# Adds of a routed unit's tiles into the output without waits between them, with spare rows for each tile

## The chip, the cores and the metric

The kernel runs on one core of a Trainium2 chip. The metric is the device time of one execution in microseconds (us). A profiled execution also has a span, from the first to the last instruction that the profile records; the device time is a little longer than the span. The engines are named as in the profile: PE (TensorE, matmuls), PEld (its weight loads), DVE (VectorE), ACT (ScalarE), POOL (GpSimd) and SP (SyncE, which here only issues DMAs). A name such as POOLq is the engine's sequencer, which handles waits and branches.

## What is computed

Four sequences of 512 tokens of 256 numbers go through a gated feed-forward stage with one expert of weights for each sequence, attention with 16 query heads over one shared key and value head, and a residual. Then comes a routed feed-forward layer with 8 experts, whose result is added to the output:

```
x = x + attn(cond(x))                      # (4, 512, 256)
xg = mixed(x).reshape(8 groups, 256 tokens, 256)
probs = softmax(xg @ w_router)             # 8 experts; each token chooses its best 2
each group sends at most 128 tokens to an expert (capacity)
h = gelu(tokens_of_expert @ wi[e])         # 256 -> 1024
y = h @ wo[e]                              # 1024 -> 256
out[token] = x[token] + sum over its chosen experts of probs[token, e] * y
```

So every token is handled by up to two experts, and its output row gets up to two additions on top of the row that the attention stage wrote.

## The kernel before

**Stages.** Up to about 390 us the kernel computes the gated feed-forward stage, the projections and the attention of the four sequences, interleaved, and scatters each token's row into a DRAM table `xp` sorted by expert (`scattered` and `numbered`, L826 to L863, by indirect DMAs from POOL at L850). From about 383 us on it runs the routed units.

**Routed units.** A unit (`routed`, L1064) is a run of rows of one expert in `xp`: 256 rows for "first", "early" and "pair" units, and 96 to 320 rows (`SIZES`, L38) for the eight "last" units, which take what is left of each expert. The list of units is at L1376 to L1380; the very last unit, ("last", 3) with 224 rows, has buffers of its own (names ending in `_alone`) and runs after a conditional block. A unit loads its expert's weights `wi` and `wo` and its rows `xt`, turns the rows by PE transposes into `xTr` (L1143, copied by DVE at L1147), makes `h` in `up` (PE at L1170, ACT at L1174) and the result in `put` (PE at L1236 into `psC`). `go` (L1258) runs `up` of unit t, the transposes of unit t+1, then `put` of unit t-1, so `put` lags by one unit. A unit has two or three tiles of up to 128 rows: 320 rows are 128, 128 and 64; 224 are 128 and 96; 192 are 128 and 64.

**Handing a tile over.** For each tile `i` of `m` rows, `out` (L1206) calls `weights` (L1189): five tiny DVE instructions (L1195 to L1199) that compute each row's factor `w0` and the output row `at` to which it is added. A row of `xp` that holds no token has the number 0; for those `at` points to spare rows behind the 2048 rows of the output: row 2048 + p for partition p, from the constant `spare1` (L211), one column for every tile. A tile of at most 64 rows also has two halves added (L1210, L1211). Then DVE scales the result into `y` (L1213) and POOL issues an indirect DMA that adds `y` to the output rows in DRAM (L1216, `compute_op=ALU.add`). After the last tile the adds end in DRAM and the program ends.

**What orders the adds.** The scheduler takes every indirect DMA into `out_rows` as touching all of it, so each add waits for the landing of the add before it, by a semaphore wait on POOL ahead of the DMA. Without that wait two adds could work on the same row at the same time: rows of one expert are different tokens, but the spare rows are shared by all tiles, and a token's two experts are in different units. `apart` (L276) takes a dependence away for a named group; `behind` (L279) adds one by hand. `y`, `at` and the factors have two buffers each in turn (pool `fp`), so a unit's DVE work waits for the adds of the unit two before it.

**The conditional block.** At L1477 every engine reads the flag `over`, and at L1478 a block for rows that did not fit is skipped in this input. Behind it, `last_go` runs the last unit. On the skipping path POOL first waits until all its earlier DMAs have landed, then sets its DMA semaphores to what the block would have left.

```
a = nc.gpsimd.indirect_dma_start(                     # L1216, in out()
    out=out_rows,
    out_offset=bass.IndirectOffsetOnAxis(ap=at[0:m, i : i + 1], axis=0),
    in_=y[0:m, i, :],
    in_offset=None,
    compute_op=ALU.add,
)
```

Of the kernel before, what the change touches and what calls it, by code (L numbers as in the profile page):

```python
# [9 lines left out]
F32 = mybir.dt.float32  # L10
# [4 lines left out]
ALU = mybir.AluOpType  # L15
# [3 lines left out]
P = 128  # L19
B = 4  # L20
T = 512
NT = B * T
D = 256
# [32 lines left out]
def adaln_attn_ffn_kernel(  # L56
# [21 lines left out]
    nc = tc.nc  # L78
# [63 lines left out]
    rows = const.tile([1, B], I32, name="rows")  # L142
# [59 lines left out]
    def numbers(name, shape, pattern, base, step):  # L202
        t = const.tile(shape, F32, name=name)
        nc.gpsimd.iota(
            t, pattern=pattern, base=base, channel_multiplier=step,
            allow_small_or_imprecise_dtypes=True,
        )
        return t

    token1 = numbers("token1", [P, NCH], [[P, NCH]], 1, 1)  # L210
    spare1 = numbers("spare1", [P, 1], [[0, 1]], NT + 1, 1)  # L211
    free = numbers("free", [P, NE], [[EROWS, NE]], 0, 0)
    begin = numbers("begin", [P, NE, NG], [[EROWS, NE], [P, NG]], 0, 0)
    tens = numbers("tens", [P, NE, 4], [[0, NE], [2, 4]], 2, 0)
# [25 lines left out]
    for n in range(2):  # L240
        t = const.tile([P, P], F32, name=f"negm{n}")
        nc.gpsimd.memset(t, 0.0)
        negm.append(t)
    for n in range(B):
        t = const.tile([P, 4, 32], F32, name=f"v{n}")
# [6 lines left out]
    for n in range(4):  # L252
        t = apool.tile([P, 4, T], F32R, name=f"qq{n}")
# [20 lines left out]
    scatters, last_rows, adds = [], [], []  # L274

    def apart(i, group, reason):  # L276
        tc.declare_no_dep(i.ins, group=group, reason=reason)

    def behind(i, others, reason):  # L279
        for k in others:  # L280
            tc.add_manual_dep(
                i.ins, k.ins.name,
                mybir.DependencyInfo(mybir.DependencyClass.Sync, mybir.DependencyReason.DATA),
                reason=reason,
            )
# [778 lines left out]
    def routed(units, alone=None):  # L1064
        def own(pool, shape, name, dt=F32, **kw):
            if alone:
                return alone.tile(shape, dt, name=f"{name}_alone", bufs=1)
            return pool.tile(shape, dt, name=name, **kw)
# [4 lines left out]
        def kind(t):  # L1073
            name, n = units[t]
            size = {"last": SIZES[n % NE], "rest": 2 * P + REST}.get(name, 2 * P)
            return lists[name], n, size

        def tiles(t):
            size = kind(t)[2]
            return [(i, min(P, size - i * P)) for i in range((size + P - 1) // P)]  # L1080
# [48 lines left out]
        def of(w, lo, n):  # L1129
            return w[:, lo // RUN, ds(lo % RUN, n)]  # L1130
# [50 lines left out]
        def put(t):  # L1181
            (expert, _), n, size = kind(t)
            k = len(tiles(t))
            w0 = own(fp, [P, 3], "w0")
            w1 = own(fp, [P, 3], "w1")
            at = own(fp, [P, 3], "at", I32)
            y = own(fp, [P, 3, D], "y")

            def weights(i, m):  # L1189
                number, e0, p0, p1 = (  # L1190
                    xt_of[t][i][0:m, DX + j : DX + j + 1] for j in range(4)
                )
                w, v = w0[0:m, i : i + 1], w1[0:m, i : i + 1]
                te = expert[0:m, n : n + 1]
                nc.vector.scalar_tensor_tensor(w, e0, te, p0, ALU.is_equal, ALU.mult)  # L1195
                nc.vector.scalar_tensor_tensor(v, e0, te, p1, ALU.not_equal, ALU.mult)  # L1196
                nc.vector.tensor_tensor(w, w, v, ALU.add)
                nc.vector.scalar_tensor_tensor(v, number, 0.0, spare1[0:m], ALU.is_equal, ALU.mult)
                nc.vector.scalar_tensor_tensor(  # L1199
                    at[0:m, i : i + 1], number, -1.0, v, ALU.add, ALU.add  # L1200
                )

            mine = []
            adds.append(mine)

            def out(i, m, p):  # L1206
                weights(i, m)
                if m <= REST:
                    other = own(fp, [REST, D], "other")
                    nc.vector.tensor_copy(other[0:m], p[REST : REST + m])  # L1210
                    nc.vector.tensor_tensor(other[0:m], p[0:m], other[0:m], ALU.add)  # L1211
                    p = other
                nc.vector.tensor_scalar(  # L1213
                    y[0:m, i, :], p[0:m], w0[0:m, i : i + 1], None, ALU.mult
                )
                a = nc.gpsimd.indirect_dma_start(  # L1216
                    out=out_rows,
                    out_offset=bass.IndirectOffsetOnAxis(ap=at[0:m, i : i + 1], axis=0),
                    in_=y[0:m, i, :],
                    in_offset=None,  # L1220
                    compute_op=ALU.add,
                )
                if units[t][0] in full_of:
                    apart(a, "last rows", "rows of other sequences")
                elif units[t] == ("pair", 0):
                    behind(a, last_rows, "the last sequence's rows")
                mine.append(a)


            outs = []  # L1230
            for i, m in tiles(t):
                if i % 2 == 0 or alone:
                    po = psC.tile([P, 2, D], F32, name="psC")
                for fc in range(F // P):
                    lo = REST * (fc % 2) if m <= REST else 0
                    mm(  # L1236
                        po[lo : lo + m, i % 2, :], hT_of[t][:, fc, ds(i * P, m)],
                        of(wo_of[t], fc * D, D),
                        start=fc == lo // REST, stop=fc >= F // P - (2 if m <= REST else 1),
                    )  # L1240
                    if fc % 4 == 3 and fc < F // P - 1:
                        yield
                outs.append((i, m, po[:, i % 2, :]))
                if alone:
                    out(*outs.pop())
                if i < k - 1:
                    yield
            for o in outs:
                out(*o)
            yield  # L1250
# [7 lines left out]
        def go(step, then=lambda: None, held=()):  # L1258
            if 0 not in xT_of:
                turn(0)  # L1260
            for t in range(N + 1):
                if t < N:
                    for _ in up(t):
                        step()
                    if t + 3 < N and t + 3 not in held:
                        fetch_in(t + 3)
                    if t + 1 < N:
                        turn(t + 1)
                    else:
                        then()  # L1270
                if t > 0:
                    for _ in put(t - 1):
                        step()
                    if t + 2 < N:
                        fetch_out(t + 2)
# [88 lines left out]
    for b in range(B):  # L1364
# [3 lines left out]
        for g in range(NE):  # L1368
            n, i = divmod((0, 64, 0, 223)[b] + (4, 4, 0, 2)[b] * g, 4)
            if b == 2:  # L1370
                n, i = thin_slots[g]
# [22 lines left out]
    for n in range(-LEAD, STEPS + 1):  # L1394
        m = n + LEAD
# [167 lines left out]
```

## Time and profile before

| | |
|---|---|
| three runs | 659.11, 659.12, 655.55 us; median 659.11 |
| the profiled execution | 654.26 us, span 652.6 us |
| mean granted TensorE clock in it | 0.977 |
| PE busy | 614.9 us, 94% of the span |
| POOL busy | 175.8 us, 27% |
| adds to the output (L1216) | 36, of 1431 to 1601 ns each on POOL |
| issue of an add to its landing | 3.2 us at least, 4.5 median, 8.5 at most |
| weights of one unit | two loads of 1024 KB |

The times come from one execution. Views used later: the chain of work that ended last (followed back from the last instruction, at each step to what released it), the timeline (instructions in order of start: start us, duration us, engine, line, operation, output<-inputs, and in brackets the idle time of the engine before it with the releaser that the profile names), and windows (busy time by engine in a stretch, with the granted clock and the DMA engines' busy share). Where the profile names a releaser for a wait on several semaphores, it is the one that came last by its records, which need not be the one that counted.

### The profile page before, as it was taken

The numbers are of one execution on the slowest core, as the hardware profiler recorded it, in microseconds if no ns is written. First come the engines' busy times: TensorE is split into PE (matmuls) and PEld (weight loads), VectorE is DVE, ScalarE is ACT, GpSimd is POOL, SyncE is SP. The second block draws the span as 40 slices with busy tenths as digits, with TensorE's granted clock in tenths as the row PEclk, the third lists the DMA queues.
The fourth block names the chain that finished last, engine by engine and source line by source line (L and its number), as shares of the span: only waits on it lengthen the run. The fifth ranks groups of instructions, "written<-read, shape, count | busy, mean of one in ns | idle before, by whom it ended". The sixth has DMA issues, their size and how long they took to land.

```text
span 652.6 us, 8247 instructions
## 1 busy us (share of the span) xinstructions
PE 614.9 (94%) x2821; PEld 404.8 (62%) x2821; DVE 340.5 (52%) x913; ACT 238.2 (36%) x430; POOL 175.8 (27%) x182
## 2 busy tenths in 40 slices
PE   8999899999999999989998499999999999999991
PEld 3445454454455555655454258888889896878880
DVE  3269886668766668988877341247212112122420
ACT  2231556555655555555545341231121112121110
POOL 7008930049000100052024240124321211121231
PEclk9999999999999999999889799999999999999997
DMA  7297375658411242232217824656667777646221
GB/s 241 75 203 267 93 227 154 181 150 251 129 53 50 83 132 54 83 105 96 57 50 255 319 92 158 195 162 188 204 176 208 242 224 194 210 116 223 24 25 20
DMA packets 65876, 97.37 MB, mean 149 GB/s; under 512 B 8290, under 2 KB 37250, under 8 KB 65794
## 3 DMA queue, kind: packets, MB, share of 16 engines
q1 hardware_dynamic: 57826, 81.72, 40.6%
q0 software_dynamic: 8000, 15.04, 9.7%
q8 instruction: 25, 0.41, 0.3%
q14 instruction: 25, 0.20, 0.1%
HBM read 67.24 MB, written 29.24 MB: 148 GB/s over the span
## 4 chain that ended last, share of the span: by engine, by line
PE 79%; DMA 11%; DVE 4%; ACT 3%; issue 1%; POOLq 0%; SPq 0%; DVEq 0%
PE psA L1170 15%; PE psC L1236 14%; PE pa L500 9%; PE pm L461 9%; PE pe L490 9%; PE side L355 7%; DMA out_dram<-y,at 7%; PE side L339 4%; PE side L386 3%; DMA inv_rows<-hl 3%; PE side L648 2%; DVE negm L463 2%; PE side L696 2%; PE pa L516 2%; ACT e L491 2%
## 5 line engine op out<-in xcount | busy, mean ns | idle before, releaser
L491 ACT ACTIVATE e<-pe 128x512 f32<-128x512 f32 x256 | 147.7, 598 | 137.4 <-PE pe L490 133.0
L463 DVE TENSOR_REDUCE negm<-pm 128x1 f32<-128x512 f32 x256 | 167.9, 684 | 55.3 <-PE pm L461 55.0
L461 PE MATMUL pm<-kk,qq 65*128 65x512 f32 x256 | 148.3, 584 | 1.6 <-DVE negm L463 1.5
L1236 PE MATMUL psC<-wo_sb,hT 128*128 128x256 f32 (+2 forms) x544 | 115.4, 381 | 1.0 <-DVE xTr L1147 1.0
L490 PE MATMUL pe<-qq,kk 67*128 67x512 f32 x256 | 108.2, 428 | 2.7 <-ACT e L491 2.2
L1170 PE MATMUL psA<-xTr,wi_sb 128*128 128x256 f32 (+5 forms) x512 | 106.4, 365 | 0.9 <-ACT hT L1174 0.9
L1174 ACT ACTIVATE hT<-psA 128x512 f32<-128x512 f32 (+3 forms) x72 | 38.9, 544 | 183.3 <-PE psA L1170 183.3
L1236 PEld LDWEIGHTS psC<-wo_sb,hT 128*128 128x128 f32 (+2 forms) x544 | 93.2, 182 | 17.3 <-issue 1.7
L1216 POOL DMA_INDIRECT out_dram<-y,at x34 | 52.2, 1536 | 179.0 <-DVE w L1196 67.8
L1170 PEld LDWEIGHTS psA<-xTr,wi_sb 128*128 128x128 f32 x512 | 90.6, 191 | 14.5 <-issue 1.2
L461 PEld LDWEIGHTS pm<-kk,qq 65*128 65x128 f32 x256 | 49.3, 192 | 56.0 <-issue 21.1
L490 PEld LDWEIGHTS pe<-qq,kk 67*128 67x128 f32 x256 | 49.4, 193 | 36.1 <-ACT e L491 26.0
L500 PE MATMUL pa<-e,v 128*32 128x512 f32 x512 | 64.7, 625 | 0.0
L355 PE MATMUL side<-xT_sb,w 128*128 128x512 f32 x128 | 62.2, 595 | 2.2 <-DMA w<-in_wcond_dram 1.4
L1213 DVE TENSOR_SCALAR y<-psC,w 128x256 f32<-128x256 f32 (+1 forms) x30 | 14.4, 481 | 72.1 <-PE psC L1236 72.1
L850 POOL DMA_INDIRECT xp<-x,to_i x32 | 32.9, 1027 | 61.2 <-DVE negm L463 34.2
L1147 DVE COPY xTr<-psC 128x512 f32<-128x512 f32 (+5 forms) x18 | 10.5, 593 | 71.8 <-PE psC L1143 71.8
L577 POOL TENSOR_TENSOR x<-x,bo_sb 128x256 f32<-128x256 f32 x16 | 12.0, 767 | 116.7 <-DMA x<-in_xtok_dram 116.7
L355 PEld LDWEIGHTS side<-xT_sb,w 128*128 128x128 f32 x128 | 24.0, 190 | 18.3 <-issue 9.5
L500 PEld LDWEIGHTS pa<-e,v 128*32 128x32 f32 x512 | 13.9, 113 | 31.7 <-issue 31.1
L339 PE MATMUL side<-hid,w 128*128 128x512 f32 x64 | 31.7, 594 | 0.3 <-DVE hid L321 0.3
L313 DVE SCALAR_TENSOR_TENSOR u<-th,u 128x512 f32<-128x512 f32 x16 | 12.9, 809 | 21.1 <-ACT u L312 21.1
(274 smaller groups left out, 543.6 us busy)
## 6 DMA issues: line engine op xcount, KB each, us to landing
wi_sb<-in_wi_dram SPq DMA_DIRECT2D x14, 1024.0 KB
wo_sb<-in_wo_dram SPq DMA_DIRECT2D x14, 1024.0 KB
xp<-zeros SPq DMA_DIRECT2D x8, 1072.0 KB
qq<-qd SPq DMA_DIRECT2D x32, 256.0 KB
ov<-o SPq DMA_DIRECT2D x16, 256.0 KB
xt<-xp SPq DMA_DIRECT2D x15, 268.0 KB
w<-in_wcond_dram SPq DMA_DIRECT2D x12, 256.0 KB
wi_sb<-in_wi_dram POOLq DMA_DIRECT2D x3, 1024.0 KB, 9.4
```

Source lines behind the costliest of these rows:

```text
L339: mm(po, wd[:, hc, ts(dc, P)], s["hid"][:, hc, :], start=hc == 0, stop=hc == 3)
L355: mm(s["ps"], s["w"][:, ds(first + P * c, P)], s["xT"][:, c, :], start=c == 0, stop=c == 1,)
L461: mm(pm, qq[u % 4][0:KMAX, hh, ts(i, P)], kk[0:KMAX, :], start=True, stop=True)
L463: nc.vector.tensor_reduce(negm[u % 2][:, c : c + 1], pm, AX.X, ALU.max, negate=True)
L490: mm(pe, kk[0:KEXP, ts(kc, P)], qq[u % 4][0:KEXP, i, :], start=True, stop=True)
L491: nc.scalar.activation(e_of[n][:, i, :], pe, AF.Exp)
L500: mm(pa_of[u][32 * i : 32 * i + 32, :], seqs[u // 4]["v"][:, kc, :], e[:, i], start=False, stop=kc == 3,)
L850: i = nc.gpsimd.indirect_dma_start(out=xp, out_offset=bass.IndirectOffsetOnAxis(ap=to_i[:, k, ch : ch + 1], axis=0), in_=s["x3"][:, ch, :] ...
L1170: mm(ph[:, f, :], of(wi_of[t], c * F + (first + f) * P, P), xT_of[t][:, c, 0:size], start=c == 0, stop=c == 1,)
L1174: nc.scalar.activation(hT_of[t][:, ds(first, per), 0:size], ph, AF.Gelu_apprx_tanh)
L1216: a = nc.gpsimd.indirect_dma_start(out=out_rows, out_offset=bass.IndirectOffsetOnAxis(ap=at[0:m, i : i + 1], axis=0), in_=y[0:m, i, :], in ...
L1236: mm(po[lo : lo + m, i % 2, :], hT_of[t][:, fc, ds(i * P, m)], of(wo_of[t], fc * D, D), start=fc == lo // REST, stop=fc >= F // P - (2 if ...
```

## The change

Three things change together. The spare rows become three sets of 128, one for each tile of a unit, so the output tensor in DRAM grows from 2048 + 256 to 2048 + 384 rows. Within a unit, the dependences among its adds are taken away. The adds of a unit are still put behind all adds of the unit before it, by hand. In addition the DMA gets an explicit bound for its row numbers.

```diff
-    spare1 = numbers("spare1", [P, 1], [[0, 1]], NT + 1, 1)
+    spare1 = numbers("spare1", [P, 3], [[P, 3]], NT + 1, 1)
...
-                nc.vector.scalar_tensor_tensor(v, number, 0.0, spare1[0:m], ALU.is_equal, ALU.mult)
+                nc.vector.scalar_tensor_tensor(
+                    v, number, 0.0, spare1[0:m, i : i + 1], ALU.is_equal, ALU.mult
+                )
...
-            mine = []
+            mine, others = [], adds[-1] if t > 0 else []
+            same = f"unit {len(adds)}"
             adds.append(mine)
...
                     in_=y[0:m, i, :],
                     in_offset=None,
+                    bounds_check=NT + 3 * P - 1,
                     compute_op=ALU.add,
                 )
                 if units[t][0] in full_of:
                     apart(a, "last rows", "rows of other sequences")
                 elif units[t] == ("pair", 0):
                     behind(a, last_rows, "the last sequence's rows")
+
+                if mine:
+                    apart(a, same, "rows of one expert")
+                tc.add_to_no_dep_group(same, a.ins)
+                behind(a, others, "rows of other experts")
                 mine.append(a)
...
-    args.append(nc.dram_tensor("out_dram", (NT + 2 * P, D), F32, kind="ExternalOutput").ap())
+    args.append(nc.dram_tensor("out_dram", (NT + 3 * P, D), F32, kind="ExternalOutput").ap())
```

The order of the instructions on every engine stays as it was; no matmul, DVE, ACT or SP instruction is added, removed or moved. On POOL the first add of a unit waits for the landing of the adds of the unit before it, and a second or third add for its own `y`, in the first units also for a landing whose semaphore it takes over.

## The prediction

> **What bounds the kernel now.** I read three views: the shares of the page, the chain of work that ended last, and the timeline of the tail for POOL, DVE and PE. The page says that PE is busy for 94% of the span, and from 382 to 638 us the windows show it busy almost without a gap. So an add can only cost time where PE has no more work. The chain shows where that is (columns: start us, length us, what):
>
> ```profile
> 585.14 5.56 PE psC L1236 x32
> ...
> 591.48 7.92 DMA out_dram<-y,at
> ...
> 600.15 39.13 DMA out_dram<-y,at
> ...
> 640.64 3.83 DMA out_dram<-y_alone,at_alone
> ...
> 645.03 1.67 POOLq L1558
> ```
>
> From 591.48 on it isn't matmuls that decide the end but one add after the other: each waits for the landing of the one before. The first of them took 7.92 us, in a stretch (591 to 605 us) where the DMA engines were 81% busy with three 1 MB weight loads; after it POOL never catches up. PE goes on beside this chain and ends first:
>
> ```profile
> 631.34 7.08 PE L1236 MATMUL psC<-wo_sb_alone,hT_alone 128*128 128x256 f32 x32
> 635.01 0.48 DVE L1213 TENSOR_SCALAR y_alone<-psC,w_alone 128x256 f32<-128x256 f32 x1 [4.83 <-PE psC L1236]
> 638.46 0.48 DVE L1213 TENSOR_SCALAR y_alone<-psC,w_alone 96x256 f32<-96x256 f32 x1 [2.15 <-PE psC L1236]
> ```
>
> The last matmul ends at 638.42 and the last `y` is ready at 638.94. In 638.5 to 652.6 us PE is busy 0.00 us. What POOL does with those tiles (L1216, one line for each add):
>
> ```profile
> 605.37 1.56 POOL L1216 DMA_INDIRECT out_dram<-y,at  x1 [3.79 <-DVE y L1213]
> 609.87 1.56 POOL L1216 DMA_INDIRECT out_dram<-y,at  x1 [2.94 <-DMA out_dram<-y,at]
> 614.49 1.43 POOL L1216 DMA_INDIRECT out_dram<-y,at  x1 [3.06 <-DMA out_dram<-y,at]
> 619.87 1.56 POOL L1216 DMA_INDIRECT out_dram<-y,at  x1 [3.94 <-DVE other L1211]
> 625.39 1.43 POOL L1216 DMA_INDIRECT out_dram<-y,at  x1 [3.96 <-DVE w L1197]
> 629.40 1.56 POOL L1216 DMA_INDIRECT out_dram<-y,at  x1 [2.58 <-DVEq L1478]
> 634.90 1.44 POOL L1216 DMA_INDIRECT out_dram<-y,at  x1 [3.94 <-issue]
> 640.64 1.56 POOL L1216 DMA_INDIRECT out_dram<-y_alone,at_alone  x1 [4.30 <-issue]
> 645.25 1.44 POOL L1216 DMA_INDIRECT out_dram<-y_alone,at_alone  x1 [3.05 <-DMA out_dram<-y_alone,at_alone]
> ```
>
> The reader is to see two things. Adds are 4.0 to 5.7 us apart though each occupies POOL for only about 1.5 us; the DVE names in brackets are only what last happened by the records, since those tiles were ready long before. And the last add starts at 645.25, 6.31 us after its `y`. What follows the last add (its landing and the program's closing) takes 652.6 - 645.25 = 7.35 us.
>
> **The change, part by part.** *Waits inside a unit.* I lay the adds out anew, by three rows. An add that waits for nothing but its `y` starts 0.28 us after it (`y` from 560.11 for 0.48 us, the add at 560.87). Two POOL DMAs without a landing between them follow at the length of the first plus 0.30 us (the eight scatters at L850, from 450.38 on, 1.29 us apart at 0.98 each, one add ahead of them). A landing comes 4.5 us after issue in the median, 8.5 at most, by the group of adds.
>
> - Unit ("last", 5), `y` ready at 617.82 and 619.92: its adds go at 618.10 and 620.20 (before: 619.87, 625.39), landed by 624.7.
> - Unit ("last", 2), `y` ready at 624.92 and 626.16: 625.20, then 625.20 + 1.56 + 0.30 = 627.06 (before: 629.40, 634.90), landed by 631.6.
> - The skipped block: POOL waits for all landings and sets semaphores; by the chain, from 639.28 to 640.64, that is 1.36 us after the landing. So POOL is free for the last unit at 633.0.
> - Last unit, `y` ready at 635.49 and 638.94: its adds go at 635.77 and 638.94 + 0.28 = 639.22 (before: 640.64, 645.25).
>
> So the last add starts 645.25 - 639.22 = 6.03 us earlier: 4.87 us because the backlog behind it is gone, 1.16 us because the two last adds no longer wait for each other but only for their tiles. Every earlier add is off the path, covered by PE's matmuls to 638.42: with the longest landing of the whole group (8.5 us) behind the add at 627.06, POOL is free at 635.56 + 1.36 = 636.92, the next add ends at 636.92 + 1.56 + 0.30 = 638.78, still ahead of 639.22. After that the bound is PE, then one DVE instruction, one add and the close; what is late next is the last `y`.
>
> *The waits that stay.* A unit's first add waits for all adds of the unit before it. Queued behind it on POOL are only the unit's other adds (and, near 450 us, the scatters of the last sequence; PE waits for none of them, it is busy 176.6 of 178.0 us from 382 to 560). From the last `y` of a unit to the first of the next are 5.0 us at the least in the tail (619.92 to 624.92) and 0.28 + 4.5 = 4.8 to the landing, so this wait is just met. Were that landing one of 8.5 us, the next adds would go at 629.4 and 631.3, POOL would be free at 631.3 + 4.5 + 1.36 = 637.1, and the add after it would end at 639.0: still ahead of 639.22.
>
> *Spare rows.* `spare1` becomes 128x3. The 128x1 generation (L204 on POOL) takes 137 ns and the 128x9 one 174 ns, so under 0.04 us more, at the start, where POOL's work is ahead of nobody who waits on it. L1198 reads one column as before. 128 more rows in DRAM move no bytes. All 0.
>
> *The explicit bound.* The trace of before shows no add with a bound. The nearest rows are on either side: the scatters at L850 are indirect DMAs of 128 rows with a bound, 0.98 to 1.03 us in this stretch; the adds without one are 1.43 to 1.56. If the bound is what makes the scatters short, an add gets 0.57 us shorter, and one such step lies on the path. If it costs, it costs less than a scatter takes altogether, 0.98 us. I take 0, since the adding and not the bound is the more likely difference between the two rows, and keep -0.57 and +0.98 for the range. The register that holds the bound is filled ahead of the wait.
>
> *A rule that speaks against it.* First the rows: the add at 560.87 lasted 1.55 us with DVE busy beside it to 561.84, and the one at 609.87 lasted 1.56 with DVE idle beside it, so DVE's work did not lengthen it. The Trainium skill, "GPSIMD Engine Reference", section Key points, says that GpSimd shares its SBUF interfaces with VectorE and contends with some DVE modes, which would make adds slower that now start right behind `y`, while DVE works on the next tile. By that rule the sum would lose nothing on the last add, beside which DVE has nothing left, and it can only feed the slower rival below; the trace does not agree so far.
>
> *The sum.* 652.6 - 6.03 = 646.6 us of span. The profiled execution took 654.26 - 652.6 = 1.66 us around its span, so 648.2 us against its own 654.26. That execution stands 4.85 us under the median of the three runs (659.11); the fastest of them is 655.55. The same 6.03 us taken from the median gives 653.1 us, my forecast.
>
> **The rivals.**
>
> *Adds in a unit do not overlap although the wait is gone* (GpSimd, or the queue, finishes one add's transfer before it starts the next). Then the spacing of 4.0 to 5.7 us stays, the backlog too, and the time is 659.1. For it: no two adds are in flight together anywhere in the trace. Against it: the scatters go out every 1.29 us while a scatter takes 2.9 us to land (median of its group), so the same queue does hold several.
>
> *The bound shortens the adds.* The last add and so its landing come 0.57 us sooner: 653.1 - 0.57 = 652.5 us. For it: the 0.98 us of the scatters. Against it: those copy and do not add.
>
> *Slower: each add gets longer on POOL*, by the bound or by work beside it. Place: the last add, which then has nothing to hide behind. It costs its own lengthening, once, since the earlier ones are covered; the gain is lost when one add takes 1.44 + 6.03 = 7.5 us, and at 14 us the time is 653.1 + 12.6 = 665.7. For it: nothing measured with a bound and an addition together. Against it: 0.98 us with a bound, 1.6 at most without, over 36 adds and 32 scatters.
>
> **How the numbers follow.** The forecast gets 0.74, no overlap 0.12, shorter adds 0.10, slower 0.04. A measurement of this kernel can tell a difference of about 1%, 6.6 us, from no change. The forecast's 6.03 us are 0.91% of 659.11, just inside; but the runs before are up to 3.56 us apart, and a median after that falls to the lower level would read as 9.6 us, so I give 0.28 of the 0.74 to faster by over 1% and 0.46 to within. Shorter adds (6.6 us) give 0.08 and 0.02, no overlap 0.12 within, slower 0.04. Together: faster 0.36, within 1% 0.60, slower 0.04. The range goes from 648.0 (the profiled execution's sum, close to 655.55 less the forecast and the shorter add, 649.0) to 657.0 (the forecast with the bound's worst 0.98 is 654.1; the rest reaches toward the rival without overlap, whose own 659.1 stays outside).
>
> **What would show it.** In the profile after, the adds of ("last", 5) and ("last", 2) should start within 0.5 us of their `y` or 1.9 us after the add before them; the last two should start near 635.8 and 639.2, and the chain should end in PE L1236, DVE L1213 and one add instead of a run of adds. POOL's idle time until a landing (24.2 us from 560 us on) should nearly go. PE should end where it ended. I am wrong if the last add starts more than 1 us after its `y`, if adds of a unit stay 4 us apart, if an add on POOL is not 1.4 to 1.6 us long, or if more than 7.35 us follow the last add.

## The result, and the profile after

| | before | after |
|---|---|---|
| median of 16 runs each, us | 654.63 | 649.24 |
| lowest to highest, us | 649.94 to 659.12 | 646.58 to 652.88 |
| ratio after / before | | 0.9919, 95% interval 0.9894 to 0.9944 |
| profiled execution: device time, span, us | 654.26, 652.6 | 652.07, 650.5 |
| mean granted clock in it | 0.977 | 0.977 |
| end of the last matmul, us | 638.42 | 642.32 |
| from there to the end of the span ("tail" below), us | 14.16 | 8.16 |

The kernel is faster by 0.8%, which is within 1%; the means of the two sets of 16 are 5.2 us apart (standard error 0.9). Ratios here and below use, of each kernel, the runs within 1.5% of its fastest; in the set of the bound alone, the spare rows alone and the last four units that leaves out 13 of the 35 runs of the kernel before, one of them of 901.91 us, which the mean given below for that set leaves out too. The forecast was 653.1 us in a range of 648.0 to 657.0.

The two spans differ by only 2.1 us, though the tail is 6.0 us shorter: the last matmul of this execution came 3.9 us later. Both are explained below. First the chain of work that ended last, in the kernel after, from 585 us on (start us, length us, what). No landing of an add stands in it any more (the view goes by the first of the last two adds):

```profile
629.11 6.29 PE psA L1170 x32
635.40 3.47 PE psC L1245 x16
638.87 0.02 issue
638.90 0.48 DVE y_alone L1216
...
640.17 1.56 POOL out_dram L1219
641.73 1.15 issue
642.88 1.68 POOLq L1567
```

The timeline of POOL in the kernel after, for its last nine adds (L1219 is before's L1216; the bracket is POOL's idle time ahead and the releaser that the profile names):

```profile
608.61 1.56 POOL L1219 DMA_INDIRECT out_dram<-y,at  x1 [9.17 <-DVE w L1196]
610.47 1.56 POOL L1219 DMA_INDIRECT out_dram<-y,at  x1 [0.30 <-DVE at L1201]
612.34 1.43 POOL L1219 DMA_INDIRECT out_dram<-y,at  x1 [0.31 <-issue]
622.50 1.56 POOL L1219 DMA_INDIRECT out_dram<-y,at  x1 [8.73 <-DVE w L1196]
624.63 1.43 POOL L1219 DMA_INDIRECT out_dram<-y,at  x1 [0.56 <-DVE w L1196]
629.61 1.56 POOL L1219 DMA_INDIRECT out_dram<-y,at  x1 [3.55 <-DVE w L1196]
631.47 1.45 POOL L1219 DMA_INDIRECT out_dram<-y,at  x1 [0.30 <-issue]
640.17 1.56 POOL L1219 DMA_INDIRECT out_dram<-y_alone,at_alone  x1 [7.25 <-DVE w_alone L1198]
643.11 1.44 POOL L1219 DMA_INDIRECT out_dram<-y_alone,at_alone  x1 [1.38 <-DVE y_alone L1216]
```

Where a unit's tiles are ready together, its adds now stand 1.86 us apart (608.61, 610.47, 612.34): the length of one plus 0.30 us. Before, the same three stood 4.5 and 4.6 us apart. Ahead of every unit POOL is idle for 3.5 to 9.2 us: the backlog is gone. The last tile on DVE and the end of PE, in the timelines of those two engines:

```profile
642.36 0.48 DVE L1216 TENSOR_SCALAR y_alone<-psC,w_alone 96x256 f32<-96x256 f32 x1 [2.16 <-PE psC L1245]
```

```profile
635.24 7.08 PE L1245 MATMUL psC<-wo_sb_alone,hT_alone 128*128 128x256 f32 x32
```

The last `y` is ready at 642.84, the last add starts at 643.11, 0.27 us later (before: 6.31 us later), and 7.37 us follow it. The length of an add, in the costliest groups of the page after (busy us, mean ns of one):

```profile
L1219 POOL DMA_INDIRECT out_dram<-y,at x34 | 52.3, 1537 | 174.0 <-DVE w L1196 152.6
```

Before it was 1536 ns.

### The profile page after: what moved, and what is told of

Same layout as the page of the kernel before. It is cut to its first block, busy times and chain, and to the rows that moved or that the text cites. A ratio compares the mean times of both kernels' runs of the same rounds, so it can differ in the third digit from the quotient of the medians.

```text
span 650.5 us, 8270 instructions
## 1 busy us (share of the span) xinstructions
PE 619.9 (95%) x2812; PEld 409.0 (63%) x2821; DVE 338.6 (52%) x913; ACT 239.0 (37%) x430; POOL 175.7 (27%) x182
## 5 line engine op out<-in xcount | busy, mean ns | idle before, releaser
L1170 PE MATMUL psA<-xTr,wi_sb 128*128 128x256 f32 (+5 forms) x512 | 109.2, 371 | 4.1 <-ACT hT L1174 4.1
L490 PE MATMUL pe<-qq,kk 67*128 67x512 f32 x256 | 110.0, 434 | 2.8 <-ACT e L491 2.3
L1170 PEld LDWEIGHTS psA<-xTr,wi_sb 128*128 128x128 f32 x512 | 92.4, 194 | 18.7 <-ACT hT L1174 4.3
L1219 POOL DMA_INDIRECT out_dram<-y,at x34 | 52.3, 1537 | 174.0 <-DVE w L1196 152.6
L355 PE MATMUL side<-xT_sb,w 128*128 128x512 f32 x128 | 64.0, 610 | 1.7 <-DMA w<-in_wcond_dram 0.9
L500 PE MATMUL pa<-e,v 128*32 128x512 f32 x512 | 62.4, 605 | 0.0
L1216 DVE TENSOR_SCALAR y<-psC,w 128x256 f32<-128x256 f32 (+1 forms) x30 | 14.4, 481 | 73.0 <-PE psC L1245 70.5
L1147 DVE COPY xTr<-psC 128x512 f32<-128x512 f32 (+5 forms) x18 | 10.5, 593 | 75.4 <-PE psC L1143 71.3
L696 PE MATMUL side<-wb,rT 128*128 128x264 f32 x64 | 18.9, 421 | 5.1 <-ACT rT L685 5.1
```

Of the source, the lines that this page charges most:

```text
L355: mm(s["ps"], s["w"][:, ds(first + P * c, P)], s["xT"][:, c, :], start=c == 0, stop=c == 1,)
L490: mm(pe, kk[0:KEXP, ts(kc, P)], qq[u % 4][0:KEXP, i, :], start=True, stop=True)
L500: mm(pa_of[u][32 * i : 32 * i + 32, :], seqs[u // 4]["v"][:, kc, :], e[:, i], start=False, stop=kc == 3,)
L1170: mm(ph[:, f, :], of(wi_of[t], c * F + (first + f) * P, P), xT_of[t][:, c, 0:size], start=c == 0, stop=c == 1,)
L1219: a = nc.gpsimd.indirect_dma_start(out=out_rows, out_offset=bass.IndirectOffsetOnAxis(ap=at[0:m, i : i + 1], axis=0), in_=y[0:m, i, :], in ...
```

## The experiments

What had to be told apart: **theory A**, the gain is the tail, made of the backlog (removed by freeing the adds of units ahead of the last) and the spacing of the last pair; its main rival **B**, the gain comes from the spare rows or the bound, by an effect on the adds themselves. Later two more pairs came up: whether the edits move pauses of PE in the middle of the kernel (E) or the chip does (F), and whether time saved in the tail can be paid for by a lower granted clock (H) or not (I). Each set of four kernels ran on one chip, beside its own runs of the kernel before (the ratios are to those). "Tail" is from the end of the last matmul to the end of the span, each from one profiled execution; unlike the time, it leaves out what shifts the end of PE as a whole. The errors given for means are standard errors.

**The whole change once more.** No edit.

> The changed kernel itself, so that the stretch from the end of the last matmul to the end of the span (call it the tail) can be compared with that of the kernels below on one chip. It was 652.58 - 638.42 = 14.16 us before and 650.46 - 642.36 = 8.1 us in the profile after. Theory A (the end was set by adds that wait for each other's landings): 8.0 to 8.3 us again, whatever the clock does ahead of it, and a time about 6 us under before. Theory D (the time also changed ahead of the tail, where PE ended 3.9 us later in the profile after): PE again ends later than before at the same granted clock, and the gain is 2 to 4 us.

Measured: 648.25 us against 653.23, ratio 0.9936 (0.9903 to 0.9969). Tail 8.08 us. The tail repeats, although PE ended 5.2 us earlier than in the first profile after, and 1.3 us earlier than in the profile before, so D gets no support, though there was less half clock ahead of it (17.1 us against 20.5). The means are 4.5 us apart (0.7), between D's 2 to 4 and A's 6.

**Spare rows and bound, with all the waits.**

```diff
-                if mine:
-                    apart(a, same, "rows of one expert")
-                tc.add_to_no_dep_group(same, a.ins)
```

> The spare rows of each tile and the explicit bound are kept; all waits between the adds of a unit are back. Theory A: nothing of the gain is left, tail 13.8 to 14.6 us, ratio 1.00. Theory B (what cost time was that tiles of a unit added into the same spare rows of DRAM, so that landings were slow): most of the gain is there, tail near 8 to 10 us, and a landing comes clearly sooner than 4.5 us after issue.

Measured: 655.53 us, ratio 1.0026 (0.9992 to 1.0059), tail 14.22 us. The gain is gone whole (the mean is even 2.2 us above that of the kernel before, 0.7), so B falls: what counts is the waits.

**Only the last unit free**, so that the backlog stays.

```diff
-                if mine:
+                if mine and alone:
```

> Only the two adds of the last unit do not wait for each other; every other add waits as before. Theory A: the backlog stays, so the first of them starts where it did (2.2 us after the end of the last matmul) and the second 1.86 us behind it: tail 14.16 - 4.61 + 1.86 = 11.4 us. Theory C (only the last pair matters, since only there PE covers nothing): tail 8.1 us, the whole gain.

Measured: 651.77 us, ratio 0.9962 (0.9932 to 0.9993), tail 11.60 us against 11.4 expected. POOL's timeline in this kernel:

```profile
636.41 1.45 POOL L1219 DMA_INDIRECT out_dram<-y,at  x1 [3.74 <-issue]
642.22 1.56 POOL L1219 DMA_INDIRECT out_dram<-y_alone,at_alone  x1 [4.37 <-issue]
644.09 1.45 POOL L1219 DMA_INDIRECT out_dram<-y_alone,at_alone  x1 [0.30 <-issue]
```

The last matmul ended at 639.77 here. The pair stands 1.87 us apart, but starts 2.45 us behind the matmuls, because the adds of the unit before were late.

**Only the last unit waiting**, all others free.

```diff
-                if mine:
+                if mine and not alone:
```

> The waits are gone in every unit but the last, whose second add waits for the landing of its first. Theory A: no backlog, the first of the two starts 0.3 to 0.8 us after its y, the second 4.6 us later: tail 14.16 - 4.87 = 9.3 us. Theory C: hardly a gain, tail 13 us or more.

Measured: 650.19 us, ratio 0.9941 (0.9912 to 0.9971), tail 9.69 us against 9.3 expected. The pair again:

```profile
634.38 1.56 POOL L1219 DMA_INDIRECT out_dram<-y_alone,at_alone  x1 [7.62 <-DVE w_alone L1198]
638.92 1.44 POOL L1219 DMA_INDIRECT out_dram<-y_alone,at_alone  x1 [2.98 <-DMA out_dram<-y_alone,at_alone]
```

No backlog is left (7.62 us idle ahead), and the last add waits for the landing of the first, 4.54 us behind it. The profiles so far order as theory A says: 14.2 with all waits, 11.6 and 9.7 with one part of the edit, 8.1 with both.

**The kernel before, again.** No edit; for the spread of its own tail and of the pauses.

> The kernel before, unchanged, for a second profile of it. In the six profiles so far the five kernels with spare rows and a bound have two PE pauses of 4.9 to 5.1 us ahead of L696 and 3.9 to 4.3 us ahead of L1170, at some 345 and 388 us, and the kernel before has one of 7.6 us ahead of L555 instead. Theory E (the program with the edits moves these pauses): this profile again has the one pause ahead of L555 and PE ends near 638 us. Theory F (the pauses come and go by execution or chip): it shows the two pauses, or others. Tail 14.1 to 14.3 us, ratio 1.00 either way.

Measured: 650.32 us against 649.79, ratio 0.9987 (0.9930 to 1.0044), tail 14.26 us. PE's waits showed the pause of the first profile before (7.5 us ahead of L555), as E says, but PE ended at 634.67 and not near 638.

**The bound alone**, on the kernel before.

```diff
                     in_offset=None,
+                    bounds_check=NT + 2 * P - 1,
                     compute_op=ALU.add,
```

> Only the explicit bound of the adds is put into the kernel before; all waits stay, so the tail should be 14.1 to 14.3 us. Theory E1 (the bound with its extra register moves on POOL shifts the work ahead of the tail): the two PE pauses of 5 and 4 us appear and the time is 1 to 2 us over before. Theory E2 (the spare rows do it, by moving every later tile in SBUF or the tensors in DRAM): no pauses of that kind, ratio 1.000. An add takes 1.43 to 1.60 us on POOL as without the bound.

Measured: 650.88 us, ratio 0.9946 (0.9884 to 1.0009), tail 13.92 us. The group of adds on the page of this kernel:

```profile
L1216 POOL DMA_INDIRECT out_dram<-y,at x34 | 52.2, 1536 | 179.8 <-DVE w L1196 64.2
```

1536 ns with the bound, 1536 without: it neither costs nor saves. The two pauses of E1 did not appear (one of 7.2 us ahead of L555), and the tail was 0.2 us under the range expected.

**The spare rows alone**, on the kernel before (128x3 constant, column `i`, 128 more rows; no bound, all waits).

```diff
-    spare1 = numbers("spare1", [P, 1], [[0, 1]], NT + 1, 1)
+    spare1 = numbers("spare1", [P, 3], [[P, 3]], NT + 1, 1)
```

> Only the spare rows of each tile (a constant of three columns, 128 more rows of output in DRAM) are put into the kernel before; no bound, all waits stay, tail 14.1 to 14.3 us. Theory E2: the two PE pauses of 5 and 4 us appear and the time is 1 to 2 us over before. Theory E1: they don't, ratio 1.000.

Measured: 649.85 us, ratio 1.0031 (0.9991 to 1.0072): no gain in time. But the tail was 10.91 us, and every theory had expected 14.1 to 14.3. So a kernel that keeps all the waits does not always have the long tail. The time says that it is not the spare rows; what it is, the third run of the kernel before shows below. The two pauses of E2 did not appear either (one of 7.7 us ahead of L555).

**Only the last four units free**, the earlier ones waiting.

```diff
-                if mine:
+                if mine and (alone or t >= N - 3):
```

> The waits are gone only in the last four units (two of three tiles or two, in order 128+128+64, 128+64, 128+96, 128+96 rows); everything before waits as in the kernel before. Theory A (the backlog that matters is made and carried in the last 50 us): tail 8.1 us, the whole gain. Theory G (the backlog is older and must be cleared earlier): tail 9 us or more.

Measured: tail 8.15 us, that of the whole change. The median was 645.51 us against 649.79 of the kernel before in the same set. The ratio of 1.0001 (0.9954 to 1.0048) compares unlike runs here, since it has all of this kernel's. The means are 3.0 us apart (0.8). The time alone leaves it open; the profile shows where the adds are:

```profile
596.71 1.43 POOL L1219 DMA_INDIRECT out_dram<-y,at  x1 [7.08 <-DMA out_dram<-y,at]
602.38 1.56 POOL L1219 DMA_INDIRECT out_dram<-y,at  x1 [4.23 <-DVE w L1198]
604.24 1.56 POOL L1219 DMA_INDIRECT out_dram<-y,at  x1 [0.30 <-issue]
606.11 1.43 POOL L1219 DMA_INDIRECT out_dram<-y,at  x1 [0.30 <-issue]
...
632.36 1.56 POOL L1219 DMA_INDIRECT out_dram<-y_alone,at_alone  x1 [7.25 <-DVE w_alone L1198]
635.30 1.44 POOL L1219 DMA_INDIRECT out_dram<-y_alone,at_alone  x1 [1.38 <-DVE y_alone L1216]
```

The slow add beside the weight loads (7.08 us of waiting ahead of 596.71) is still there, and it no longer matters: three adds 1.87 us apart make it up at once.

**The whole change, third time.** No edit, as the partner of the next kernel.

> The whole change, beside the three kernels below on one chip. So far its tail was 8.08 and 8.16 us, 6.0 us less than before, but the times of whole sets of runs moved by only 4.5 to 5.2 us on the mean, and in the runs the end of PE was 1.5 to 2 us later than before, with 1.5 us more time at half clock ahead of it. Theory H (the idle time of PE that the change takes from the end is partly paid back by the clock, in the next execution): mean time 4 to 5 us under before, clock-corrected end of PE as before. Theory I (chance and chip): the gain is the tail's, 5.5 to 6.5 us, within the scatter of the means (0.9 us).

Measured: 649.55 us against 652.5, ratio 0.9938 (0.9905 to 0.9972), tail 8.16 us. The means are 4.0 us apart (0.7): this is in the 4 to 5 us of theory H and under the 5.5 to 6.5 of theory I.

**The whole change with the time put back**: seven copies of 96x256 on GpSimd ahead of the very last add, which no data needs.

```diff
+                    if alone and mine:
+                        idle = alone.tile([P, D], F32, name="idle_alone", bufs=1)
+                        for _ in range(7):
+                            nc.gpsimd.tensor_scalar(idle[0:m], y[0:m, i, :], 1.0, None, ALU.mult)
```

> The whole change, and seven GpSimd copies of 96x256 ahead of the very last add, which do nothing for the result and give the tail back its old length with PE idle: some 0.8 us each, so tail 13.7 to 14.7 us. Theory H: PE's time at half clock ahead of its end falls back to that of before and the time is that of before. Theory I: the time at half clock stays that of the whole change, and the time is that of the whole change plus 5.6 to 6.6 us, whatever before has.

Measured: 655.02 us, ratio 1.0026 (0.9995 to 1.0057), tail 14.62 us. Against the whole change of the same set the mean is 5.9 us higher (655.36 and 649.50, standard error of the difference 0.9), for a tail 6.5 us longer.

```profile
636.52 1.56 POOL L1225 DMA_INDIRECT out_dram<-y_alone,at_alone  x1 [7.25 <-DVE w_alone L1198]
639.29 6.44 POOL L1222 TENSOR_SCALAR idle_alone<-y_alone 96x256 f32<-96x256 f32 x7 [1.20 <-DVE y_alone L1216]
645.89 1.50 POOL L1225 DMA_INDIRECT out_dram<-y_alone,at_alone  x1 [0.16 <-issue]
```

So a microsecond ahead of the last add is worth about a microsecond of device time (5.9 for 6.5), as theory I has it (5.6 to 6.6). The half clock ahead of PE's end was 20.5 us in the profiles of both kernels, where theory H has it fall back to that of the kernel before (13.7 us in the profile of this set, next). By H the mean time would be that of the kernel before (653.50); it lies 1.9 us above (0.8). So H is unlikely but not ruled out: each kernel has one profile in this set, and the tail here is longer than those of the kernel before.

**The kernel before, third time.** No edit.

> The kernel before, for a third profile of its tail, which was 14.16 and 14.26 us in two profiles, 14.22 and 13.92 us in two kernels that keep the waits and 10.91 us in a third. Theory J (with the waits the tail depends on what each landing meets, such as a 16 KB fetch of instructions on one of the DMA engines): again 10.5 to 14.5 us, and where it is short, fewer landings have one late part. Ratio 1.00.

Measured: 653.10 us, ratio 0.9988 (0.9957 to 1.0019), and a tail of 11.37 us: the kernel before itself has both tails. Here the last matmul ended at 638.74, within 0.3 us of the first profile before, so the adds can be laid beside those that the prediction shows:

```profile
614.68 1.43 POOL L1216 DMA_INDIRECT out_dram<-y,at  x1 [2.91 <-DMA out_dram<-y,at]
618.63 1.56 POOL L1216 DMA_INDIRECT out_dram<-y,at  x1 [2.51 <-DVE w L1196]
623.21 1.43 POOL L1216 DMA_INDIRECT out_dram<-y,at  x1 [3.02 <-DMA out_dram<-y,at]
627.03 1.56 POOL L1216 DMA_INDIRECT out_dram<-y,at  x1 [2.38 <-DVE y L1213]
632.45 1.45 POOL L1216 DMA_INDIRECT out_dram<-y,at  x1 [3.87 <-issue]
638.24 1.56 POOL L1216 DMA_INDIRECT out_dram<-y_alone,at_alone  x1 [4.34 <-issue]
642.75 1.44 POOL L1216 DMA_INDIRECT out_dram<-y_alone,at_alone  x1 [2.95 <-DMA out_dram<-y_alone,at_alone]
```

From 614.68 to 618.63 are 3.95 us, and 4.58 to the next. In the first profile before the same two steps took 5.38 (614.49 to 619.87) and 5.52 us (to 625.39). That is 2.4 of the 2.8 us by which the tails differ; the other steps repeat within 0.2 us. What differs inside those two steps is told in the last section. The tile of the add of 618.63 was this one:

```profile
617.77 0.48 DVE L1213 TENSOR_SCALAR y<-psC,w 128x256 f32<-128x256 f32 x1 [3.92 <-PE psC L1236]
```

It was ready at 618.25, 0.38 us ahead of its add: here POOL had caught up with PE before the last three units. In the first profile before, the same add was 2.04 us behind its tile (617.82, 619.87).

**All but the last four units free**, the rest waiting.

```diff
-                if mine:
+                if mine and not alone and t < N - 3:
```

> The complement of the run with the last four units alone: the waits are gone in all earlier units and stay in the last four. Theory A: the backlog starts again in the last four units, from 604 us on, where nine adds at 4.0 to 5.5 us each follow; by the lengths of before the last add starts at 641.6 to 644.0 instead of 645.25 us, so a tail of 10.5 to 12.9 us. Theory G: the backlog is made earlier, tail 9 us or less.

Measured: 654.34 us, ratio 1.0008 (0.9981 to 1.0035), tail 11.48 us, inside the 10.5 to 12.9 expected. POOL in this kernel:

```profile
608.00 1.56 POOL L1219 DMA_INDIRECT out_dram<-y,at  x1 [9.17 <-DVE w L1196]
...
621.90 1.56 POOL L1219 DMA_INDIRECT out_dram<-y,at  x1 [3.34 <-DVE w L1196]
...
641.62 1.56 POOL L1219 DMA_INDIRECT out_dram<-y_alone,at_alone  x1 [4.42 <-issue]
646.24 1.44 POOL L1219 DMA_INDIRECT out_dram<-y_alone,at_alone  x1 [3.05 <-DMA out_dram<-y_alone,at_alone]
```

POOL comes to 608.00 after 9.17 us of idling, without any backlog, and still the last add is as late as in the third profile of the kernel before (4.15 and 4.01 us behind the last matmul). So the backlog that counts is not what the slow add near 591 us leaves. Nor is it what the three adds from 608.00 on leave, for the next one starts 0.28 us behind its tile:

```profile
621.14 0.48 DVE L1216 TENSOR_SCALAR y<-psC,w 128x256 f32<-128x256 f32 x1 [3.92 <-PE psC L1245]
```

The chained adds of the last three units, six of them, build it anew. The time of this kernel is not below that of the kernel before (the mean is 0.4 us higher, 0.6).

All kernels side by side, by what is free in them:

| adds free of waits inside a unit | tails, us |
|---|---|
| none (before three times; the spare rows, the bound, or both) | 14.16, 14.26, 11.37; 10.91, 13.92, 14.22 |
| all but the last four units | 11.48 |
| the last unit only | 11.60 |
| all but the last unit | 9.69 |
| the last four units only | 8.15 |
| all (three times) | 8.16, 8.08, 8.16 |

A single tail is a sample where the waits stay, so a row alone can mislead: 11.60 for the last unit only is near the short tails of the first row. But in that profile the adds of 616.07 and 621.42 landed late as in the long-tailed ones (4.6 us each, see the last section), and its last pair stands 1.87 us apart instead of 4.5 to 4.6.

What wasn't tried on the chip: overlapping adds without the explicit bound, and freeing the last three units alone.

## Why the prediction was right, and where not

**The place and the mechanism: right.** The time was lost behind PE's last matmul and in the waits for landings, and it came back there: the tail went from 14.16 to 8.16 us, 6.00 against the 6.03 of the sum. That the two agree to 0.03 us is luck of this pair of profiles: against the third profile of the kernel before (11.37) it would be 3.21. Neither the spare rows nor the bound moved the time alone.

**The layout of the adds: right, one delay too short.** The adds of ("last", 5) and ("last", 2) start 0.28 us after their `y` (ready at 622.22, 624.35 and 629.33; adds at 622.50, 624.63 and 629.61) or 1.86 us after the add before them (631.47), as forecast. Only the first add of the last unit starts 0.79 us after its `y` (639.38, 640.17) and not 0.28. There the trace has POOL's sequencer in a wait of its own until 639.42, and the add 0.75 us behind its end; in the chain before, the same step from a landing to the add (599.44 to 600.15) took 0.71 us. What fills it was not separated. This cost nothing, since POOL was free 1.1 us ahead of the last add (640.17 + 1.56 + 0.30 = 642.03, against 643.11). The last add starts 0.27 us after its `y`, as forecast. It is followed by 7.37 us where the prediction's sign of being wrong stood at 7.35; before it was 7.33 by the trace, and all profiles have 7.27 to 7.40, so that sign was set too tight to tell anything.

**The delay at the skipped block: misread.** The prediction took 1.36 us from the landing to the next add (639.28 to 640.64). The add of 634.90 landed at 638.28 by its last semaphore update; 639.28 lies inside the 1.00 us (638.39 to 639.39) in which POOL sets the semaphores. So the delay was 2.36 us, and the chain's piece of 39.13 us is no single landing (the add of 600.15 landed 4.47 us after its start). With 2.36 us the prediction's two worst cases end at 639.8 and 640.0, behind 639.22 and not ahead of it. Neither came: in the profile after the add of 631.47 landed at 634.84, so that POOL could go on at 637.2, well ahead of 640.17.

**The two parts of the 6.03 us: right in kind.** Freeing all units but the last takes the tail from 14.16 to 9.69 us, 4.5 (forecast 4.87 for the backlog); freeing the last pair as well takes it to 8.16, another 1.5 (forecast 1.16; the first add's start 0.5 us later accounts for the difference). In the other order the last pair alone brings 2.6 and the backlog 3.4: the sum is one, its division is not.

**The rivals: none came.** Adds of a unit do overlap (1.86 us apart), and they got neither shorter nor longer (1537 ns against 1536). The Trainium skill, "GPSIMD Engine Reference", section Key points, says that GpSimd shares its SBUF interfaces with VectorE and contends with some DVE instructions. No effect of it shows here: in the profile after, the add of 608.61 with DVE busy beside it and the add of 640.17 with DVE idle from 640.19 on both took 1.56 us.

**"POOL's idle time until a landing should nearly go": right.** From 560 us on, POOL's waits before were (engine, line, releaser: us in total, times, longest)

```profile
POOL out_dram L1216 <- DMA out_dram<-y,at: 24.2, 6, 7.1
...
POOL out_dram L1216 <- DMA out_dram<-y_alone,at_alone: 3.0, 1, 3.0
```

and after, where no landing is named any more, they begin

```profile
POOL out_dram L1219 <- DVE w L1196: 59.1, 7, 15.1
POOL out_dram L1219 <- DVE w_alone L1198: 7.2, 1, 7.2
POOL out_dram L1219 <- DVE y_alone L1216: 1.4, 1, 1.4
```

**"PE should end where it ended": wrong, but not by the change as far as the runs show.** It ended 3.90 us later in the profile after. PE's waits of over 3 us there are

```profile
PE side L696 <- ACT rT L685: 5.1, 1, 5.1
PE psA L1170 <- ACT hT L1174: 4.1, 1, 4.1
```

where the profile before has one:

```profile
PE side L555 <- DMA inv_rows<-hl: 7.6, 1, 7.6
```

The kernel before itself, in its third run, shows the two of the kernel after:

```profile
PE side L696 <- ACT rT L685: 5.1, 1, 5.1
PE psA L1170 <- ACT hT L1174: 4.0, 1, 4.0
```

On the chip of the first and third set all kernels had these two, on the chip of the second set all had the one ahead of L555 (7.2 to 7.7 us, 2.2 in the kernel with the last four units free), whatever the edit. So E falls and F stands as far as two chips go; which chip the first two profiles come from is not on record, and why the pauses differ stays open. Part of the shift can be the granted clock: ahead of the last matmul the profile after was granted half clock for 27.3 us, the one before for 20.5, and the three profiles of the whole change end their matmuls at 637.12, 639.34 and 642.32 with 17.1, 20.5 and 27.3 us of it, some 0.5 us for each. By that estimate the clock makes 3.4 of the 3.9 us. It doesn't hold everywhere: the third profile of the kernel before has the same two pauses as the profile after and 13.6 us less of half clock, but ends only 3.6 us earlier, where the estimate says 6.8. A wrong step here would have spoiled a forecast made from two single executions; it doesn't touch the tail.

**The term that was mis-sized: the gain, taken from one execution with a long tail.** The prediction set 6.03 us against a tail of 14.16 as if it were a constant of the kernel, and it said that after the slow add of 591.48 POOL never catches up. It does: in the third profile of the kernel before and in the kernel with all but the last four units free, POOL was level with PE again at the first add of ("last", 5), and only six adds of backlog were left. In the first profile two late landings kept it behind. The six profiles that keep all the waits have 14.16, 14.26, 11.37, 14.22, 13.92 and 10.91, in the mean 13.1, while the change always gives 8.1. So the mean gain should be about 13.1 - 8.1 = 5.0 us, an estimate from six executions of four kernels; the differences of the means measured are 5.2, 4.5 and 4.0 us (0.9, 0.7 and 0.7).

**The time itself** came out 3.9 us below the forecast, for a reason apart from the change: the base. The three runs of before had a median of 659.11, the sixteen 654.63, 4.5 us lower. 4.5 less of base and 0.6 less of gain (6.0 forecast, 5.4 between the medians) make the 3.9. The prediction's own sum for the profiled execution, 648.2 us, was within 1.0 us of the measured median. That is luck too: the profiled execution, 654.26 us, happened to lie by the median of the sixteen runs, which nobody could tell from three.

## What to carry to other kernels

When PE is done, read the last stretch as a chain and ask of each wait in it what it protects; a wait for a landing (here 2.6 to 4.3 us of POOL's idling in the tail for a 1.5 us add) can go when the rows are made distinct, and freeing the last four units gave the whole shortening of the tail here (8.15 us, in one profile). A chain of landings also passes on every late one, so its length in a single profile is a sample: lay two or three profiles of the same kernel side by side before calling one length the price. Measure such an edit by the stage (the tail repeated within 0.1 us after the change), because the total wanders by more than the gain.

## What the runs showed of the hardware that was not expected

**One late part holds up a landing.** An add's landing consists of 16 semaphore updates. In the first profile before, the add of 614.49 had 15 of them 3.13 us after its start and the 16th at 4.62; the add of 619.87 had them at 3.82 and 4.78. Beside each stands a fetch of instructions among the DMA transfers (from 616.55 for 1.48 us, from 621.99 for 1.47 us). In the second profile before the same two had the 16th at 4.43 and 4.67, again beside such fetches (1.55 and 1.40 us). Each of these four late parts came 1.1 to 1.2 us after the end of its fetch. In the third, with the short tail, both adds landed whole at 3.20 and 3.83 us; a fetch stands beside the first of them too (from 615.00 for 0.93 us), but it ended 1.25 us after the add's start, before any part had landed. Counting gaps of over 0.2 us between the 15th and the 16th update from the add of 614.49 on, the six profiles that keep the waits sort by it: 2.0 to 2.5 us in all in the four with tails of 13.9 to 14.3 us, none in the two with 11.4 and 10.9. The Trainium skill, "DMA: Bandwidth & Descriptors", section on why a DMA increments its semaphore by 16 and not by 1, says that only the full count means that all data have landed. In these traces POOL waits for the full count: the next adds start 0.75 us after the 16th update (619.11 to 619.87, 624.64 to 625.39). That the fetch is what delays the part is the coincidence of these records, and was not tested by itself. The kernel after has a late part too (add of 624.63: 3.09 and 3.79 us), and nothing waits there.

**The end of a program is long.** 7.3 to 7.4 us follow the start of the last add in every profile, whether one or two adds were in flight.

**The run-to-run spread goes with the granted clock.** The sixteen runs after reach from 646.58 us at a mean clock of 0.987 to 652.88 at 0.977. The stretches of half clock in the middle of the kernel are 3.4, 6.8 or 10.2 us long (13.7 in one profile), and profiles differ in how many they have. Estimated from the runs' mean clocks, a run of the whole change spent 23.0 to 23.7 us at half clock and one of the kernel before 27.5 to 28.0 on one chip (1.2 and 0.7). The tail can account for that difference: it has 2.7 to 3.3 us of it in the profiles of the whole change and 6.4 to 11.2 in those of the kernel before. On the other chip the kernel with only the last four units free and the kernel before spent the same, 24.5 and 24.2 us (0.9 each), though the tail of the first has 5.2 us of it and those of the three kernels there that keep the waits 6.0 to 11.2; so there the first seems to have spent more of it ahead of the last matmul. Why stays open; it would go some way to account for the gain of only 3.0 us there.
